# TensorE's order in the attention written out by hand up to block 12, and the residual's transposes three blocks late

## The chip, the cores and the metric

The kernel runs on one core of a Trainium2 chip. The metric is the device time of one execution in microseconds, as the median of several runs. A core has five engines, each with its own queue: TensorE (PE; its weight loads are shown apart as PEld), VectorE (DVE), ScalarE (ACT), GpSimd (POOL) and SyncE (SP), which issues nearly all DMAs. TensorE writes its results to PSUM[...]; VectorE and ScalarE read them from there.

## The reference

One transformer block on `x` of 2048 x 1024, in fp32, with one attention head of width 256 and a gated feed-forward part of width 2752:

```python
x = x + layernorm(attention(layernorm(x), Wqkv, bqkv, Wo, bo))
x = x + layernorm(ffn(layernorm(x), W_gate, W_up, W_down))

# attention
q, k, v = split(x @ Wqkv + bqkv)
out = softmax(q @ k.T / 16) @ v
return out @ Wo + bo
# ffn
return (silu(x @ W_gate.T) * (x @ W_up.T)) @ W_down.T
```

## The kernel before

Every fp32 operand of a matmul is held as a pair, a rounded high part and the low part that is left (`split`: a copy on ScalarE, line 109, and a subtraction on VectorE, line 110). A product of two such operands is three matmuls, hi·hi, hi·lo, lo·hi (`mm3`, lines 144 to 148). Where the output is narrow (256 columns, `attend`), hi·hi and hi·lo are one matmul of 512 columns (line 276) and lo·hi one of 256 (line 277).

The kernel has these stages. From 0 to about 155 us the rows of `x` are normalised, transposed, and multiplied to q, k and v; the last four `v_block`s come just after the first block's scores. Then the attention runs over 16 blocks of 128 query rows (the loop of line 899). After it comes the feed-forward part, all through line 605, in two halves of the rows, with Strassen-like sums of its operands; it fills the rest up to 1693 us.

In one pass of the loop, block `i` does this:

- `turn(i, j)`, j = 0 to 3: four transposes on TensorE (line 268) of the exponentials `p_s` into bank 4 or 7, then a `split` into `pT`.
- `scores(i + 1, j)`: six matmuls (lines 146 to 148) of the next block's query rows with 512 keys into bank j, and the row maximum on VectorE (line 251).
- `softmax(i + 1)`: small operations on VectorE, four exponentials on ScalarE (line 259) from banks 0 to 3 into `p_s`, the sum and its reciprocal (lines 260 and 261).
- `turn_o(i - 1)`: two transposes (line 285) of the block before's output into bank 5, and a `split` into `oTs`.
- `attend(i)`: 32 matmuls into bank 6; then ScalarE copies one half of the bank (line 279) and VectorE adds the other (line 280).
- `proj(i - 1)`: two halves of six matmuls each, the first into bank 5, the second into bank 7, each followed by an eviction on VectorE that scales and adds the bias (line 295).
- `xpose(i - 2)` for the first eight blocks (`EARLY`): eight transposes (line 347) of the finished rows into banks 6 and 5, a copy on ScalarE for each bank (line 349), and a store to `xT_d` (line 351).
- `residual(i - 1)` for the first eight blocks: bn_stats (line 116), aggregates (119, 120), a power on GpSimd (121), a normalisation on ScalarE (303), the addition of `x` (304), and the same once more for the second layernorm (308). The rows lie in three pairs of buffers (`pair`), used in turn.
- `first_sums` and `first_load` in later blocks load the transposed rows back (line 361) and form the feed-forward part's first operands (lines 384 and 407, 408).

The Python order of the calls isn't the order on the engines. A scheduler reorders all instructions by its own estimate of when each can run, under the data dependencies; only instructions marked with `tc.keep_in_program_order` keep their order among themselves on their engine. In the kernel before no attention matmul is marked, and the scheduler weaves pieces of `attend`, `scores`, `turn`, `proj` and `xpose` into each other. On each engine the woven order is then fixed; an instruction waits on semaphores of others. Buffers and banks are named by the kernel, so a bank that is written again waits for its last reader.

## Time and profile before

| | us |
|---|---|
| median of 3 runs (lowest to highest) | 1696.84 (1696.13 to 1699.03) |
| the profiled execution | 1695.4 |
| its span, first to last instruction | 1693.5 |
| mean granted TensorE clock | 0.996 |
| first transpose of `p_s` on TensorE | at 163.04 |
| last matmul of `attend(15)` begins | at 439.84 |
| last gap on TensorE between attention and feed-forward part ends | at 464.66 |

How to read its lines. On the page, busy time is given per engine with its share of the span and its count of instructions; the chain follows, from the last instruction backwards, what released each step. A line of the view by stretch has the stretch, its length, then for each engine the busy time and in brackets the instructions begun in it, then the granted clock, the share of the DMA engines and GB/s. A line of the waits has the waiting instruction, who released it, the sum of the idle time in us, how often, and the longest. A line of the timeline has start and duration in us, engine, source line, operation, output and input with shapes, count, and in brackets the idle time before it and who ended it. In all views a number of a line of the kernel (L276) is a number of the listing above; in the changed kernel the same lines stand eight or more further down.

### The profile page before, as it was taken

The numbers are of one execution on the slowest core, as the hardware profiler recorded it, in microseconds if no ns is written. First come the engines' busy times: TensorE is split into PE (matmuls) and PEld (weight loads), VectorE is DVE, ScalarE is ACT, GpSimd is POOL, SyncE is SP. The second block draws the span as 40 slices with busy tenths as digits, with TensorE's granted clock in tenths as the row PEclk, the third lists the DMA queues.
The fourth block names the chain that finished last, engine by engine and source line by source line (L and its number), as shares of the span: only waits on it lengthen the run. The fifth ranks groups of instructions, "written<-read, shape, count | busy, mean of one in ns | idle before, by whom it ended". The sixth has DMA issues, their size and how long they took to land.

```text
span 1693.5 us, 21093 instructions
## 1 busy us (share of the span) xinstructions
PE 1669.1 (99%) x7764; PEld 1385.6 (82%) x7764; DVE 1098.7 (65%) x1682; ACT 695.1 (41%) x1039; POOL 91.2 (5%) x118
## 2 busy tenths in 40 slices
PE   8999999999899999999999999999999999999997
PEld 6888887888688888888888888888888888888886
DVE  8643667667687777777578447966555665445458
ACT  3222445544544444444355444433333333344343
POOL 1000000000001111111000000100000000000001
PEclk9999999999999999999999999999999999999999
DMA  6221123335655666666567655633332223666654
GB/s 214 81 81 38 38 75 112 100 115 178 211 175 199 205 207 231 216 211 223 175 215 254 209 191 193 212 118 115 130 105 94 93 94 124 217 215 194 193 191 158
DMA packets 131014, 271.00 MB, mean 160 GB/s; under 512 B 13280, under 2 KB 29792, under 8 KB 130912
## 3 DMA queue, kind: packets, MB, share of 16 engines
q1 hardware_dynamic: 128176, 262.72, 46.5%
q10 hardware_dynamic: 2736, 6.95, 1.2%
q8 instruction: 60, 0.98, 0.2%
q14 instruction: 42, 0.34, 0.1%
HBM read 185.73 MB, written 83.89 MB: 159 GB/s over the span
## 4 chain that ended last, share of the span: by engine, by line
PE 94%; DVE 2%; issue 1%; DMA 1%; ACT 1%; POOL 0%; POOLq 0%; DVEq 0%; SPq 0%; ACTq 0%
PE bank L605 71%; PE bank L147 4%; PE bank L146 4%; PE bank L148 4%; PE bank L276 3%; PE bank L277 2%; PE bank L206 2%; PE bank L268 1%; PE bank L207 1%; PE bank L347 1%; PE bank L139 1%; DVE small L116 1%; PE bank L784 0%; PE bank L785 0%; DMA f<-x 0%
## 5 line engine op out<-in xcount | busy, mean ns | idle before, releaser
L605 PE MATMUL bank<-a 128*128 128x512 f32 x1164 | 274.2, 389 | 0.0
L605 PEld LDWEIGHTS bank<-a 128*128 128x128 f32 x1164 | 218.5, 188 | 45.4
L605 PE MATMUL bank<-xb,a 128*128 128x512 f32 x912 | 212.1, 389 | 0.0
L605 PEld LDWEIGHTS bank<-xb,a 128*128 128x128 f32 x912 | 171.1, 188 | 35.5
L110 DVE TENSOR_TENSOR a<-f2p,a 128x1024 fp32r<-128x1024 f32 (+2 forms) x133 | 134.6, 1012 | 57.7 <-ACT a L109 53.7
L109 ACT CAST a<-f2p 128x1024 fp32r<-128x1024 f32 (+2 forms) x133 | 117.5, 884 | 127.4 <-PE bank L605 103.9
L110 DVE TENSOR_TENSOR a<-f,a 128x1024 fp32r<-128x1024 f32 (+2 forms) x91 | 91.1, 1001 | 105.7 <-ACT a L109 103.7
L605 PE MATMUL bank<-wvo 128*128 128x512 f32 x612 | 149.6, 389 | 0.0
L605 PE MATMUL bank<-kx,a 128*128 128x512 f32 x612 | 146.3, 389 | 0.0
L605 PE MATMUL bank<-a,a 128*128 128x512 f32 x588 | 140.1, 390 | 0.9 <-ACT xi L661 0.9
L605 PEld LDWEIGHTS bank<-kx,a 128*128 128x128 f32 x612 | 114.8, 188 | 24.1 <-ACT a L109 0.3
L605 PEld LDWEIGHTS bank<-wvo 128*128 128x128 f32 x612 | 114.9, 188 | 23.9
L605 PEld LDWEIGHTS bank<-a,a 128*128 128x128 f32 x588 | 110.2, 188 | 24.6 <-ACT xi L661 1.4
L109 ACT CAST a<-f 128x1024 fp32r<-128x1024 f32 (+2 forms) x91 | 69.6, 764 | 139.3 <-PE bank L605 108.1
L618 DVE TENSOR_TENSOR p_s<-bank,p_s 128x512 f32<-128x512 f32 x96 | 65.1, 682 | 78.4 <-PE bank L605 43.2
L605 PE MATMUL bank<-a,wvo 128*128 128x512 f32 x444 | 106.2, 389 | 0.0
L605 PE MATMUL bank<-kx,wvo 128*128 128x512 f32 x420 | 100.1, 389 | 0.0
L276 PE MATMUL bank<-a,a 128*128 128x512 f32 x256 | 94.8, 403 | 4.2 <-ACT f L349 2.1
L110 DVE TENSOR_TENSOR wvo<-f,wvo 128x1024 fp32r<-128x1024 f32 (+1 forms) x52 | 60.7, 1168 | 56.8 <-ACT wvo L109 56.5
L605 PEld LDWEIGHTS bank<-a,wvo 128*128 128x128 f32 x444 | 83.3, 188 | 17.3
L605 PEld LDWEIGHTS bank<-kx,wvo 128*128 128x128 f32 x420 | 78.8, 188 | 16.4
L121 POOL TENSOR_TENSOR small<-small,mhalf 128x1 f32<-128x1 f32 x48 | 38.0, 792 | 702.6 <-DVE small L120 670.7
(245 smaller groups left out, 2772.5 us busy)
## 6 DMA issues: line engine op xcount, KB each, us to landing
f2p<-wgu SPq DMA_DIRECT2D x41, 512.0 KB, 5.3
f<-x SPq DMA_DIRECT2D x30, 512.0 KB, 3.9
hd_S<-p_s SPq DMA_DIRECT2D x60, 256.0 KB, 4.5
f<-wgu SPq DMA_DIRECT2D x22, 512.0 KB, 3.5
wr<-wgu SPq DMA_DIRECT2D x21, 512.0 KB, 5.7
f<-wd SPq DMA_DIRECT2D x20, 512.0 KB, 5.0
hd_A<-xi SPq DMA_DIRECT2D x40, 256.0 KB, 2.0
td_T<-f SPq DMA_DIRECT2D x40, 256.0 KB, 4.5
```

The source lines that it names most:

```text
L109: nc.scalar.copy(hi, src)
L110: (lo_engine or nc.vector).tensor_tensor(lo, src, f32(hi), ALU.subtract)
L116: b = nc.vector.bn_stats(s[:, 6 * i : 6 * i + 6], h)
L121: nc.gpsimd.tensor_tensor(s[:, 15:16], s[:, 14:15], mhalf, ALU.pow)
L146: nc.tensor.matmul(o, w[0], m[0], start=first, stop=False)
L147: nc.tensor.matmul(o, w[0], m[1], start=False, stop=False)
L148: nc.tensor.matmul(o, w[1], m[0], start=False, stop=last)
L206: nc.tensor.matmul(b, xg[:, c, 0, cols], wv_s[:, c, :, :].rearrange("p a f -> p (a f)"), start=(c == 0), stop=False)
L276: nc.tensor.matmul(b, p[:, k, 0, :], vt[:, k, :, :].rearrange("p h d -> p (h d)"), start=(k == 0), stop=False)
L277: nc.tensor.matmul(b[:, D:], p[:, k, 1, :], vt[:, k, 0, :], start=False, stop=(k == NKB - 1))
L605: one = nc.tensor.matmul(o, w[i], m[j], start=first and n == 0, stop=last and n == 2, skip_group_check=chained)
L618: nc.vector.tensor_tensor(o, a, b, op)
```

## The change

A marker `pin` is passed to the attention's matmuls and transposes. While `block[0]`, which the loop sets to `i`, is under 13, it marks them with `tc.keep_in_program_order`; in the last three passes it does nothing. (The scores of block 0 are never marked; those of block 13 are issued in pass 12 and are.) Three things move in the loop: `xpose` comes a block later and in front of `turn(i, 2)`, with its two banks exchanged; `turn_o` comes before the load of `x`; `q_load` moves from the start of the passes 4 and 8 to the middle of the passes 5 and 9. The second half of `proj` goes to bank 6 in place of bank 7. The name `pin` of the later code becomes `keep`. With this, TensorE's order in a block is: turns 0 and 1, the next scores 0 and 1, the transposes of `xpose(i - 3)`, turns 2 and 3, scores 2 and 3, `turn_o(i - 1)`, `attend(i)`, `proj(i - 1)`.

```diff
-    def mm3(o, w, m, first, last):
-
-        nc.tensor.matmul(o, w[0], m[0], start=first, stop=False)
-        nc.tensor.matmul(o, w[0], m[1], start=False, stop=False)
-        nc.tensor.matmul(o, w[1], m[0], start=False, stop=last)
+    def mm3(o, w, m, first, last, pin=lambda i: i):
+
+        pin(nc.tensor.matmul(o, w[0], m[0], start=first, stop=False))
+        pin(nc.tensor.matmul(o, w[0], m[1], start=False, stop=False))
+        pin(nc.tensor.matmul(o, w[1], m[0], start=False, stop=last))
...
+    ORDERED = NT - 3
+    block = [0]
+
+    def pin(i):
+        return tc.keep_in_program_order(i) if block[0] < ORDERED else i
+
+    free = lambda i: i
...
-            mm3(bank[j], (q[:, d, 0, cols], q[:, d, 1, cols]), (k[:, 0, :], k[:, 1, :]), d == 0, d == 1)
+            mm3(bank[j], (q[:, d, 0, cols], q[:, d, 1, cols]), (k[:, 0, :], k[:, 1, :]), d == 0, d == 1, pin if i else free)
...
-        for h, b in ((1, bank[5]), (0, bank[7])):
+        for h, b in ((1, bank[5]), (0, bank[6])):
             cols = slice(h * 512, h * 512 + 512)
             for d in range(2):
-                mm3(b, (oT[:, d, 0, :], oT[:, d, 1, :]), (wo_s[:, d, 0, cols], wo_s[:, d, 1, cols]), d == 0, d == 1)
+                mm3(b, (oT[:, d, 0, :], oT[:, d, 1, :]), (wo_s[:, d, 0, cols], wo_s[:, d, 1, cols]), d == 0, d == 1, pin)
...
     for i in range(NT):
         more = i + 1 < NT
-        if i % TB == 0 and TB <= i < NT - TB:
-            q_load(i // TB + 1)
+        block[0] = i
         turn(i, 0)
         turn(i, 1)
         if more:
             scores(i + 1, 0)
             scores(i + 1, 1)
+        if 3 <= i < EARLY + 3:
+            xpose(i - 3, *pair[(i - 3) % 3], (bank[5], bank[6]), pin)
         turn(i, 2)
         turn(i, 3)
         if more:
             scores(i + 1, 2)
             scores(i + 1, 3)
             softmax(i + 1)
+        if i > 0:
+            turn_o(i - 1)
+        if i % TB == 1 and TB < i < NT - TB:
+            q_load(i // TB + 1)
         if i < EARLY:
             nc.sync.dma_start(pair[i % 3][1], x[i * P : (i + 1) * P, :])
-        if i > 0:
-            turn_o(i - 1)
...
         attend(i)
         if i > 0:
             proj(i - 1)
-        if 2 <= i < EARLY + 2:
-            xpose(i - 2, *pair[(i - 2) % 3], (bank[6], bank[5]))
```

The transposes of `turn`, `turn_o` and `xpose` and the matmuls of `attend` get `pin(...)` around them in the same way.

More of the change, by code (lines that the diff above doesn't have):

```diff
@@ L267, in turn @@
             k = 4 * j + n
-            nc.tensor.transpose(b[:, n * P : (n + 1) * P], p_s[:, k * P : (k + 1) * P], ident)
+            pin(nc.tensor.transpose(b[:, n * P : (n + 1) * P], p_s[:, k * P : (k + 1) * P], ident))
         d = pT[i % 2][:, 4 * j : 4 * j + 4, :, :]
@@ L275, in attend @@
         for k in range(NKB):
-            nc.tensor.matmul(b, p[:, k, 0, :], vt[:, k, :, :].rearrange("p h d -> p (h d)"), start=(k == 0), stop=False)
-            nc.tensor.matmul(b[:, D:], p[:, k, 1, :], vt[:, k, 0, :], start=False, stop=(k == NKB - 1))
+            pin(nc.tensor.matmul(b, p[:, k, 0, :], vt[:, k, :, :].rearrange("p h d -> p (h d)"), start=(k == 0), stop=False))
+            pin(nc.tensor.matmul(b[:, D:], p[:, k, 1, :], vt[:, k, 0, :], start=False, stop=(k == NKB - 1)))
         o = o_s[i % 2]
@@ L284, in turn_o @@
         for d in range(2):
-            nc.tensor.transpose(b[:, d * P : (d + 1) * P], o_s[i % 2][:, d * P : (d + 1) * P], ident)
+            pin(nc.tensor.transpose(b[:, d * P : (d + 1) * P], o_s[i % 2][:, d * P : (d + 1) * P], ident))
         split(oTs[i % 2][:, :, 0, :], oTs[i % 2][:, :, 1, :], b.rearrange("p (d q) -> p d q", d=2))
@@ L339, in block_kernel, with xpose @@
         split(wo_s[:, d, 0, :], wo_s[:, d, 1, :], f4[d])
-    def xpose(t, a, b, banks):
+    def xpose(t, a, b, banks, pin=lambda i: i):
         for hf in range(2):
@@ L346, in xpose @@
                 cb = 4 * hf + j
-                nc.tensor.transpose(o[:, j * P : (j + 1) * P], a[:, cb * P : (cb + 1) * P], ident)
+                pin(nc.tensor.transpose(o[:, j * P : (j + 1) * P], a[:, cb * P : (cb + 1) * P], ident))
             s = b[:, hf * 512 : hf * 512 + 512]
@@ L399, in build_x @@
         split_x("T4", cb, r1[:, R])
-    pin = tc.keep_in_program_order
+    keep = tc.keep_in_program_order
     def split_later(dst, src):
-        pin(nc.scalar.copy(dst[:, :, 0, :], src))
-        pin(nc.vector.tensor_tensor(dst[:, :, 1, :], src, f32(dst[:, :, 0, :]), ALU.subtract))
+        keep(nc.scalar.copy(dst[:, :, 0, :], src))
+        keep(nc.vector.tensor_tensor(dst[:, :, 1, :], src, f32(dst[:, :, 0, :]), ALU.subtract))
     def first_load(cb, r1, r2):
@@ L743, in down_weights @@
         r1, r2 = f4[0:2]
-        pin(nc.vector.tensor_tensor(r2[:, R], r2[:, R], r1[:, R], ALU.subtract))
+        keep(nc.vector.tensor_tensor(r2[:, R], r2[:, R], r1[:, R], ALU.subtract))
         add(r1[:, R], r1[:, R], r1[:, L], ALU.subtract)
```

## The prediction

> **What bounds the kernel now.** I read four views in this order: the page's shares and its chain of waits, the busy time by stretch, TensorE's waits, and the timelines of TensorE, VectorE and ScalarE between 163 us (the first transpose of `p_s`) and 466 us (where the feed-forward part runs without gaps).

> ```profile
> PE 1669.1 (99%) x7764; PEld 1385.6 (82%) x7764; DVE 1098.7 (65%) x1682; ACT 695.1 (41%) x1039; POOL 91.2 (5%) x118
> ...
> PE 94%; DVE 2%; issue 1%; DMA 1%; ACT 1%; POOL 0%; POOLq 0%; DVEq 0%; SPq 0%; ACTq 0%
> ```

> TensorE sets the end. The number and size of its matmuls do not change, so the change can only add or remove gaps. The stretches show how little there is to win:

> ```profile
> 163.00:418.00 255.00, 250.97 (x1380) 211.41 (x1379) 169.75 (x342) 121.47 (x254) 12.99 (x32) 1.00 0.30 99
> 418.00:466.00 48.00, 43.37 (x198) 34.32 (x197) 35.12 (x47) 25.93 (x37) 0.00 (x0) 1.00 0.59 204
> ```

> The third column is TensorE: 4.0 us idle in the first stretch, 4.6 us in the second. Its waits there:

> ```profile
> PE bank L276 <- ACT f L349: 2.1, 3, 1.4
> PE bank L276 <- ACT a L109: 2.1, 2, 1.4
> ...
> PE bank L146 <- DVE oTs L110: 0.5, 1, 0.5
> ```

> A gap costs more than its idle time, because a matmul of 512 columns is drawn 0.39 us long but starts 0.2266 us after its predecessor (114.26 us for 504 in the chain). So I count start to start:

> ```profile
> 274.69 0.60 PE L347 MATMUL bank<-ident,f 128*128 128x128 f32 x4
> 275.12 0.60 PE L268 MATMUL bank<-ident,p_s 128*128 128x128 f32 x4
> 275.56 0.38 PE L285 MATMUL bank<-ident,f 128*128 128x128 f32 x2
> 277.37 0.50 PE L276 MATMUL bank<-a,a 128*128 128x512 f32 x1 [1.43 <-ACT f L349]
> ```

> Ten transposes at 0.11 us should take 1.1 us less the 0.08 us that the last of a group gives to the next matmul (202.25 to 202.60 for four, and 0.31 instead of 0.2266 for the matmul after); they took 2.68: 1.67 us lost. Summed this way, the gaps of at least 0.05 us before 412 us cost 6.0 us (at 176 to 179 us 1.34; 207 0.76; 222 0.26; 239 0.64; 259 to 261 0.89; 274 1.67; 293 to 296 0.47). From 436 to 466 us another 6.5 us are lost.

> [...] at 236.40 below, an addition stands behind an instruction that waited. [...] The change puts `proj`'s second half into the bank in which `attend` has just ended; that is my main term. [...]

> **The change part by part.** I compared the instruction orders of the two built programs; they carry no times.

> *Removed.* The order that the scheduler wove (`attend` cut into pieces, transposes between) goes up to block 12, and with it the places of the 6.0 us. In the fixed order the next softmax lies beside `attend` and `proj` (5.6 + 2.7 us), and `xpose`'s data are a block older. Gain 6.0 us; from 4 (some return elsewhere) to 8 (the small excess goes too: 784 matmuls at 0.0035 us is 2.8 us).

> *Fewer groups of transposes.* 81 groups become 49. Four transposes and the matmul after take 0.35 + 0.31 = 0.66 us, which is 4 x 0.109 + 0.2266; two take 0.13 + 0.32 = 0.45, which is 2 x 0.11 + 0.2266. So the price is per transpose, not per group: nothing.

> *Later loads.* `q_load` comes a block later and the load of `x` behind it on SP; both have some ten us before their reader in the next block (store 2.3 to 5.9 us and load 3.9 us, begun near 5 us of a block of 16.7 us). Nothing; up to 1 us.

> *The added wait: bank 6.* `attend(i)` ends in bank 6; `proj(i-1)` does half 1 in bank 5 (six matmuls, 1.36 us), then half 0 in bank 6. Its first matmul waits for the addition (line 280 before, 288 after), which follows ScalarE's copy (279, after 287). How fast it can be, from quiet engines:

> ```profile
> 390.48 0.28 PE L277 MATMUL bank<-a,a 128*128 128x256 f32 x1
> ...
> 390.79 0.37 ACT L279 COPY f<-bank 128x256 f32<-128x256 f32 x1 [4.07 <-PE bank L277]
> ...
> 391.20 0.42 DVE L280 TENSOR_TENSOR f<-bank,f 128x256 f32<-128x256 f32 x1 [0.50 <-ACT f L279]
> ...
> 391.75 0.39 PE L148 MATMUL bank<-wvo,oTs 128*128 128x512 f32 x1
> ...
> 392.18 0.75 DVE L295 SCALAR_TENSOR_TENSOR f<-bank,ys,bo_s 128x512 f32<-128x512 f32 x1 [0.56 <-PE bank L148]
> ```

> The bank is free at 391.62 + 0.06 and would be wanted at 391.98: 0.3 us of room. But in the changed program VectorE's queue has the eviction of half 1 (line 303, before 295) ahead of the addition in blocks 2, 4, 5, 6, 8 and 9, and in all but block 9 a bn_stats (116) between them as well. The eviction must wait for half 1's last matmul, so half 0 cannot start with it. The trace of before has one such case, and there nobody waited for the bank:

> ```profile
> 236.40 0.75 DVE L295 SCALAR_TENSOR_TENSOR f2p<-bank,ys,bo_s 128x512 f32<-128x512 f32 x1 [2.32 <-PE bank L148]
> 237.06 0.42 DVE L280 TENSOR_TENSOR f<-bank,f 128x256 f32<-128x256 f32 x1
> 237.39 0.69 DVE L116 BATCH_NORM_STATS2 small<-f2p 128x6 f32<-128x512 f32 x1
> 237.99 0.68 DVE L110 TENSOR_TENSOR a<-bank,a 128x512 fp32r<-128x512 f32 x1
> ```

> From the moment when half 0 wants to start: 0.20 until the eviction starts (391.98 to 392.18), 0.66 until the next may start (236.40 to 237.06), 0.60 for bn_stats (237.39 to 237.99), 0.42 for the addition, 0.06 to TensorE (207.89 to 207.95), and 0.1 for each small op of the softmax between. Block 2: 2.1; 4, 5, 6 and 8: 2.0 each; 9: 1.4. Sum 11.5 us, on the path because TensorE's next instruction is that matmul and the order is fixed. Bounds: 10 (no small ops) and 14 (ScalarE's copy late too: in blocks 4, 5 and 8 four exponentials and a 1.24 us activation stand ahead of it).

> *Block 10.* Four sums of `first_sums` (line 392) precede the addition on VectorE and wait for loads. Before, the first of them ran 8.34 us after `xpose`'s last copy (343.28 to 351.62). That copy ends about 5.3 us into the block, so the sums start near 13.6, take 4 x 0.6 and small ops, and the addition ends near 16.7 where 15.3 is wanted: 1.4 us (0 to 4).

> *Block 0.* `wo`'s two splits wait for the last `v_block` matmuls and stand on VectorE ahead of the evictions of the transposes; the fourth transpose group waits for bank 7, by the durations about 0.9 us (0 to 1). Blocks 3 and 7 have the addition first, after late exponentials: 0.1 each.

> *The tail.* Blocks 13 to 15 stay woven. By `attend(15)`'s end the new program has done 40 feed-forward matmuls and the old one 50; the other 10 (2.3 us) then cover waits of the 6.5 us. I take 2 us off (6.5 off to 2 on).

> Sum: 11.5 + 1.4 + 0.9 + 0.2 - 6.0 - 2.0 = +6.0 us. The profiled execution took 1695.4 us, 1.9 more than its span, so 1701.4; the median 1696.84 lies 1.4 above it, and with it the forecast is 1702.8.

> **The rivals.** (1) The tail absorbs the delay, so the time is not slower: the preparations between 436 and 466 us do not depend on TensorE's delay and all 6.5 us go. Then +1.5 us, 1698.3. For it: the chain there passes two DMA waits (5.20 and 4.52 us). Against: the buffers of those loads are freed by the same blocks. It decides from 4.6 us absorbed. (2) The fixed order wins: the lost 6.0, all of the tail's 6.5 and the 2.8 of small excess go, and the bank waits cost only their lower bound, 10: -4 to -5, 1692. Against: three bounds at once. (3) Late VectorE work pushes on: exponentials and loads in blocks 9 to 12 come late as well, 5 us more, 1708. For it: in a residual block VectorE has some 11 us of work in 16.7 us, and 1.24 us activations sit ahead of splits. (4) The order isn't kept as written: excluded, the built order shows it.

> **How the numbers follow.** Forecast 0.52, rival 1 0.23, rival 2 0.11, rival 3 0.14. 0.2% is 3.4 us, about what a measurement of this kernel can tell from no change. Slower takes rival 3 and nearly all of the forecast, 0.65; same takes rival 1 and the forecast's low edge, 0.23; faster 0.12. The range goes from 1695 (between rivals 1 and 2) to 1708 (rival 3); the forecast's own range is 1699 to 1706.

> **What would show it.** TensorE's waits: the proj matmul of line 146 released by VectorE's line 288, six times or more, near 2 us each, 9 us or more in all; the waits on line 357's copies (349 before) gone from the attention; VectorE idle before line 303 (a wait on line 148), with line 288 after it. I am wrong if line 288's waits sum to less than 4 us, or if the span between 418 and 466 us loses its gaps.

## The result, and the profile after

The changed kernel takes 1712.67 us (median of 5 runs, 1710.39 to 1715.57) against 1696.84 us of the kernel before (5 runs, 1695.99 to 1699.03). The ratio is 1.0091, with an interval of 1.0080 to 1.0102: slower by 15.8 us. The forecast was 1702.8 with a range of 1695 to 1708; the direction was right, the size lies outside the range. The profiled execution took 1710.6 us with a span of 1708.6 us, 15.1 more than before; the sums below are made against that. Only this run was profiled, and it is one of the two shortest. The granted clock listed for the five runs falls as they get longer, from 0.994 and 0.993 (1710.55 and 1710.39 us) to 0.990 (1715.57 us). A stretch of 3.41 us at half clock, of which more below, lowers that mean by 0.001 (3.41 / 2 in 1710 us), so the median run, at 0.991, probably holds more of them than the profiled one; that is an estimate.

The page and its chain say the same as before: the same 7764 matmuls, TensorE at the end, and a lower share of it.

```profile
PE 1673.3 (98%) x7764; PEld 1389.5 (81%) x7764; DVE 1097.9 (64%) x1682; ACT 693.5 (41%) x1039; POOL 91.2 (5%) x118
...
PE 94%; DVE 2%; DMA 2%; ACT 1%; issue 1%; POOL 0%; SPq 0%; POOLq 0%; DVEq 0%; ACTq 0%
```

The view by stretch shows where the time went:

```profile
163.00:418.00 255.00, 240.15 (x1296) 202.55 (x1295) 155.29 (x320) 113.08 (x238) 13.00 (x32) 0.98 0.28 90
418.00:466.00 48.00, 46.17 (x230) 37.70 (x230) 37.14 (x57) 24.40 (x41) 0.00 (x0) 1.00 0.54 187
```

In the attention's 255 us TensorE is now idle for 14.9 us where it was 4.0, begins 1296 matmuls and transposes where it began 1380, and its granted clock, 1.00 before, is 0.98. The second stretch is not comparable line by line, since the attention ends later in it. TensorE's waits name the causes:

```profile
PE bank L146 <- DVE f L288: 12.2, 7, 2.0
PE bank L276 <- DVE f L211: 2.7, 1, 2.7
```

The first is the wait for bank 6 (one of the kernel's eight tiles of 128 x 512 fp32 in PSUM, line 77) that the prediction was about: seven times, at 217, 253, 272, 293, 330, 350 and 368 us, which are blocks 2, 4, 5, 6, 8, 9 and 10. The waits on line 349's copies (357 now), 2.1 us before, are gone from the attention. Here is one of the seven, in block 5, from the timeline of PE, VectorE and ScalarE (lines left out where marked):

```profile
269.34 1.25 ACT L316 ACTIVATE f<-f,small 128x1024 f32<-128x1024 f32 x1
269.50 0.16 DVE L268 TENSOR_REDUCE ys<-ys 128x1 f32<-128x4 f32 x1 [2.85 <-ACT p_s L267]
...
269.73 0.39 PE L148 MATMUL bank<-wvo,oTs 128*128 128x512 f32 x1
270.16 0.75 DVE L303 SCALAR_TENSOR_TENSOR f<-bank,ys,bo_s 128x512 f32<-128x512 f32 x1 [0.50 <-PE bank L148]
270.47 0.38 ACT L287 COPY f<-bank 128x256 f32<-128x256 f32 x1
...
270.94 0.69 DVE L116 BATCH_NORM_STATS2 small<-f 128x6 f32<-128x512 f32 x1
271.55 0.41 DVE L288 TENSOR_TENSOR f<-bank,f 128x256 f32<-128x256 f32 x1
272.01 0.50 PE L146 MATMUL bank<-wvo,oTs 128*128 128x512 f32 x1 [1.90 <-DVE f L288]
...
273.28 0.60 PE L148 MATMUL bank<-wvo,oTs 128*128 128x512 f32 x1
273.68 1.91 PE L276 MATMUL bank<-ident,p_s 128*128 128x128 f32 x8
...
275.24 0.78 PE L146 MATMUL bank<-kx,qb 128*128 128x512 f32 x1
```

The reader sees the queue that the prediction described: the last matmul of proj's half 1 starts at 269.73, its eviction (L303) at 270.16, bn_stats (L116) at 270.94, and only then the addition that frees bank 6 (L288) at 271.55. Half 0 could have started at 269.96 (269.73 + 0.2266) and starts at 272.01. ScalarE's copy (L287) ended at 270.85 and was not the last.

The lower part shows something that the prediction did not have. From 273.30 to 276.71 us matmuls took twice as long: eight transposes take 1.56 us from start to start of what follows (273.68 to 275.24), where 8 x 0.109 less 0.08 gives 0.79. (The drawn durations end later than that; only starts are counted here.) The stretches that begin after the gaps of block 4 and of block 5 differ in one column, the granted clock:

```profile
252.90:256.20 3.30, 3.16 (x18) 2.68 (x19) 1.49 (x4) 1.00 (x2) 0.00 (x0) 1.00 0.00 0
273.40:276.80 3.40, 3.40 (x14) 2.91 (x13) 2.68 (x4) 1.17 (x2) 0.00 (x0) 0.51 0.03 5
```

After three of the seven gaps (blocks 5, 6 and 8) TensorE ran for 3.41 us at half clock, that is, at a granted clock of 0.50, from 273.30, 293.78 and 331.32 us. Counted from start to start, against 0.2266 us for a matmul of 512 columns and 0.109 for a transpose, that cost 1.6 us each time.

The second wait, in block 0, is larger than predicted. The transposes of `turn(0, 1)` go to bank 7, which holds the last `v_block`, and the addition that reads it out (L211) stands behind two splits on VectorE:

```profile
169.72 1.22 DVE L110 TENSOR_TENSOR wvo<-f,wvo 128x1024 fp32r<-128x1024 f32 x1
170.86 0.68 DVE L110 TENSOR_TENSOR a<-bank,a 128x512 fp32r<-128x512 f32 x1
171.46 0.41 DVE L211 TENSOR_TENSOR f<-bank,f 128x256 f32<-128x256 f32 x1
...
172.02 0.63 PE L276 MATMUL bank<-ident,p_s 128*128 128x128 f32 x4 [2.67 <-DVE f L211]
```

The balance of the two profiled executions, from start to start on TensorE:

| term | predicted, us | measured, us |
|---|---|---|
| gaps of the woven order, gone | -6.0 | -6.5 |
| bank 6 in blocks 2, 4, 5, 6, 8, 9 | 11.5 | 12.4 |
| bank 6 in block 10 | 1.4 | 1.6 |
| bank 6 in blocks 3 and 7 | 0.2 | 0.25 |
| block 0 | 0.9 | 2.9 |
| half clock after three gaps | none | 4.9 |
| tail (from 436 us) | -2.0 | -0.9 |
| after TensorE's last matmul | none | 0.4 |
| sum | +6.0 | +15.1 |

The last line but one is no wait of TensorE: the last matmul begins at 1683.66 us before and at 1698.35 after, 14.7 us later, and the span ends 15.1 later.

### The profile page after: what moved, and what is told of

Its sections match the earlier page's. It is cut to its first block, busy times and chain, and to the rows that moved or that the text cites. A ratio compares the mean times of both kernels' runs of the same rounds, so it can differ in the third digit from the quotient of the medians.

```text
span 1708.6 us, 21083 instructions
## 1 busy us (share of the span) xinstructions
PE 1673.3 (98%) x7764; PEld 1389.5 (81%) x7764; DVE 1097.9 (64%) x1682; ACT 693.5 (41%) x1039; POOL 91.2 (5%) x118
## 4 chain that ended last, share of the span: by engine, by line
PE 94%; DVE 2%; DMA 2%; ACT 1%; issue 1%; POOL 0%; SPq 0%; POOLq 0%; DVEq 0%; ACTq 0%
PE bank L613 70%; PE bank L146 4%; PE bank L148 4%; PE bank L147 4%; PE bank L284 3%; PE bank L276 2%; PE bank L285 2%; PE bank L206 1%; PE bank L355 1%; PE bank L207 1%; PE bank L139 1%; DVE small L116 1%; PE bank L792 0%; PE bank L793 0%; DMA f<-wgu 0%
## 5 line engine op out<-in xcount | busy, mean ns | idle before, releaser
L613 PE MATMUL bank<-a 128*128 128x512 f32 x1164 | 274.2, 389 | 0.0
L613 PEld LDWEIGHTS bank<-a 128*128 128x128 f32 x1164 | 218.5, 188 | 45.4
L613 PE MATMUL bank<-xb,a 128*128 128x512 f32 x912 | 212.5, 389 | 0.0
L613 PEld LDWEIGHTS bank<-xb,a 128*128 128x128 f32 x912 | 170.9, 188 | 35.4
L110 DVE TENSOR_TENSOR a<-f2p,a 128x1024 fp32r<-128x1024 f32 (+2 forms) x133 | 134.5, 1012 | 58.9 <-ACT a L109 55.0
L109 ACT CAST a<-f2p 128x1024 fp32r<-128x1024 f32 (+2 forms) x133 | 117.4, 884 | 130.7 <-PE bank L613 101.2
L110 DVE TENSOR_TENSOR a<-f,a 128x1024 fp32r<-128x1024 f32 (+2 forms) x91 | 91.5, 1005 | 105.9 <-ACT a L109 103.7
L613 PE MATMUL bank<-wvo 128*128 128x512 f32 x612 | 149.6, 389 | 0.0
L613 PE MATMUL bank<-kx,a 128*128 128x512 f32 x612 | 146.9, 390 | 1.6 <-ACT kx L415 1.1
L613 PE MATMUL bank<-a,a 128*128 128x512 f32 x588 | 140.0, 389 | 0.9 <-ACT xi L669 0.9
L613 PEld LDWEIGHTS bank<-kx,a 128*128 128x128 f32 x612 | 114.6, 188 | 26.2 <-ACT kx L415 1.5
L613 PEld LDWEIGHTS bank<-wvo 128*128 128x128 f32 x612 | 114.9, 188 | 23.9
L613 PEld LDWEIGHTS bank<-a,a 128*128 128x128 f32 x588 | 110.2, 188 | 24.6 <-ACT xi L669 1.3
L109 ACT CAST a<-f 128x1024 fp32r<-128x1024 f32 (+2 forms) x91 | 69.6, 765 | 141.9 <-PE bank L613 106.9
L613 PE MATMUL bank<-a,wvo 128*128 128x512 f32 x444 | 106.2, 389 | 0.0
L613 PE MATMUL bank<-kx,wvo 128*128 128x512 f32 x420 | 100.1, 389 | 0.0
L613 PEld LDWEIGHTS bank<-a,wvo 128*128 128x128 f32 x444 | 83.3, 188 | 17.3
L110 DVE TENSOR_TENSOR wvo<-f,wvo 128x1024 fp32r<-128x1024 f32 (+1 forms) x52 | 60.8, 1169 | 56.0 <-ACT wvo L109 55.4
L613 PEld LDWEIGHTS bank<-kx,wvo 128*128 128x128 f32 x420 | 78.8, 188 | 16.4
```

The source lines that it names most:

```text
L109: nc.scalar.copy(hi, src)
L110: (lo_engine or nc.vector).tensor_tensor(lo, src, f32(hi), ALU.subtract)
L613: one = nc.tensor.matmul(o, w[i], m[j], start=first and n == 0, stop=last and n == 2, skip_group_check=chained)
```

## The experiments

Theory A was that the waits for bank 6 and for block 0's bank, and the half clock that came after three of the five longer ones (1.90 to 1.96 us), are the whole loss, and that the fixed order is a gain once the banks are free. Its rivals: the order itself costs time; bank 6 alone costs it; the half clock has nothing to do with the gaps. Line numbers are those of the changed kernel. Each kernel was compared with runs of the kernel before on the same chip (1696.8 to 1697.2 us).

**Another bank for proj's second half (bank 1).** Bank 1 holds a quarter of the next block's scores, which the second of the four exponentials reads while `attend` runs.

```diff
-        for h, b in ((1, bank[5]), (0, bank[6])):
+        for h, b in ((1, bank[5]), (0, bank[1] if block[0] < ORDERED else bank[6])):
```

> proj's second half goes to bank 1 in the marked passes; all else as in the changed kernel. Theory A (the loss is the wait for bank 6, and the slow clock follows from its gaps): the waits of line 146 on line 288 go (14.3 us counted start to start), no stretch of half clock is left in the attention (4.9 us), and bank 1 is free in time because its exponentials end before the first half of proj does. 1712.7 - 19.2 = 1693.5, with 1692 to 1697 allowed for the tail. Theory B (the fixed order and the late transposes cost by themselves): 1703 or more, the gaps return at other places.

Measured: 1692.66 us (1690.14 to 1695.94), ratio 0.9975 (0.9968 to 0.9981), span 1689.7. No wait on line 288 is left:

```profile
163.00:418.00 255.00, 252.33 (x1392) 215.76 (x1391) 169.91 (x346) 121.62 (x256) 13.08 (x32) 0.99 0.31 101
171.28:174.69 3.41, 2.89 (x9) 2.54 (x10) 1.49 (x4) 0.99 (x2) 0.00 (x0) 0.50 0.49 154
```

The 2.7 us of idle time in the first stretch are block 0's wait. One point of the expectation failed: a stretch of half clock is left, the second line, right after that wait. (In the changed kernel the same wait brought none; the last section says why. It brought one in the two kernels with bank 7 and with the addition first, too, from 172.6 and 172.9 us.) One bank, with the rest of the change kept, takes 20 us off and makes the kernel faster than before. So most of the loss is in the bank, and with this bank the order is a gain. Bank 1 in the woven order was not tried.

**The bank of before (bank 7) in the fixed order.**

```diff
-        for h, b in ((1, bank[5]), (0, bank[6])):
+        for h, b in ((1, bank[5]), (0, bank[7])):
```

> proj's second half goes to bank 7, as before the change; the order stays marked. Theory A: no waits on line 288, but the next block's second group of transposes (bank 7, 0.4 us after proj's end) now waits for the eviction of that half: 0.2 + 0.75 + 0.06 - 0.44 = 0.6 us in each of 12 blocks, 7 us in all, too short for the clock to drop. 1700, 1697 to 1704. Theory B: as in the changed kernel or slower, 1710 or more.

Measured: 1704.87 us, ratio 1.0052 (1.0037 to 1.0067). TensorE's waits:

```profile
PE bank L276 <- DVE f L303: 5.2, 7, 1.4
PE bank L276 <- DVE f L211: 2.7, 1, 2.7
PE bank L276 <- ACT a L109: 2.1, 3, 0.7
```

With the old bank the wait moves to the next block: its transposes into bank 7 (L276) come right after proj and wait for the eviction (L303). Eleven such places lose about 10 us from start to start, over the 7 expected, and the time lies just above the expected range. None of these waits (1.4 us at most) was followed by half clock. So in a fixed order without free room bank 7 is no way out either: with the bank of before, the fixed order and the moves make the kernel 8.0 us slower.

**No block marked.** All other parts of the change are kept, and the scheduler weaves as before.

```diff
-    ORDERED = NT - 3
+    ORDERED = 0
```

> Nothing is marked (the scheduler orders all blocks), but the moved calls and bank 6 stay. Theory A: the scheduler weaves other matmuls between the end of attend and the second half of proj, so bank 6 costs little: 1694 to 1700, as before the change. Theory B: the moved calls and the bank carry part of the loss without any marking: 1703 to 1712.

Measured: 1697.36 us, ratio 1.0007 (0.9998 to 1.0015). The moved `xpose`, `turn_o` and `q_load`, and bank 6, cost nothing that could be measured when TensorE's order isn't fixed. The trace has one stretch of half clock, and it follows two shorter gaps (1.01 and 0.53 us, waits on the feed-forward part's splits), not one long one:

```profile
442.40:445.80 3.40, 1.86 (x7) 0.97 (x6) 2.88 (x5) 3.17 (x4) 0.00 (x0) 1.00 0.87 231
445.80:449.20 3.40, 3.40 (x9) 2.56 (x8) 3.09 (x5) 1.92 (x4) 0.00 (x0) 0.50 1.02 392
```

**Bank 6 alone in the kernel before.**

```diff
-        for h, b in ((1, bank[5]), (0, bank[7])):
+        for h, b in ((1, bank[5]), (0, bank[6])):
```

> The kernel before with proj's second half in bank 6 in place of 7 and nothing else of the change. Theory A (the wait comes from the bank together with the fixed order: a scheduler that knows of the bank puts other work between attend and the second half): the same as before within 2 us, 1697 (1695.5 to 1699), waits on line 280 under 3 us in all. Rival B (the bank alone makes the wait): six or more waits of 1 us or more on line 280 and 1704 or more.

Measured: 1697.88 us, ratio 1.001 (1.0001 to 1.0018). There is no wait on line 280 (288 in the changed kernel) among TensorE's; the first ones in the attention are those of the woven order:

```profile
PE bank L276 <- ACT f L349: 2.1, 5, 0.7
...
PE bank L276 <- DVE f L295: 0.9, 1, 0.9
PE bank L276 <- ACT a L109: 0.7, 1, 0.7
```

So bank 6 and the moves cost next to nothing without the fixed order (about 1 us at most in the medians), while the fixed order costs 15.8 us with bank 6, 8.0 with bank 7 and nothing with bank 1. What costs is the wait for a bank in an order that can't go round it.

**The addition ahead of the eviction on VectorE.** The two operations are marked too, so that they keep the program's order.

```diff
-        nc.vector.tensor_tensor(o, b[:, D:], o, ALU.add)
+        pin(nc.vector.tensor_tensor(o, b[:, D:], o, ALU.add))
...
-            nc.vector.scalar_tensor_tensor(a[:, cols], b, ys[i % 4][:, 13:14], bo_s[:, cols], ALU.mult, ALU.add)
+            pin(nc.vector.scalar_tensor_tensor(a[:, cols], b, ys[i % 4][:, 13:14], bo_s[:, cols], ALU.mult, ALU.add))
```

> Bank 6 stays; VectorE's addition after attend and proj's evictions are marked too, so that the addition stands ahead of the first half's eviction. Theory A, with VectorE's queue as the cause: the waits on line 288 shrink to what ScalarE's copy leaves (it ends late behind exponentials and a 1.25 us activation): about 1.4 us in blocks 4, 5, 8 and 9, 1.2 in block 2, 1.3 in block 10, little elsewhere, 8.5 us instead of 14.3; with gaps of 1.4 us the clock does not drop (4.9 us more). 1702, 1699 to 1706. If the clock drops all the same: 1707. If the queue's order does not matter: 1712.

Measured: 1705.57 us, ratio 1.0057 (1.0042 to 1.0072), at the upper end of what was expected. The waits on line 288 are still seven but shorter, and the timeline of block 5 says why they do not go:

```profile
270.99 1.25 ACT L316 ACTIVATE f<-f,small 128x1024 f32<-128x1024 f32 x1
...
272.12 0.38 ACT L287 COPY f<-bank 128x256 f32<-128x256 f32 x1
272.53 0.42 DVE L288 TENSOR_TENSOR f<-bank,f 128x256 f32<-128x256 f32 x1 [1.03 <-ACT f L287]
...
273.01 0.50 PE L146 MATMUL bank<-wvo,oTs 128*128 128x512 f32 x1 [1.21 <-DVE f L288]
```

With VectorE's queue out of the way, the same bank waits for ScalarE's: its copy (L287) stands behind the exponentials and a normalisation of 1.25 us (L316). It is so in the other blocks too: VectorE waited for line 287 before line 288 eight times, 9.2 us in all. Two queues held the bank, and the prediction's upper bound for the term (ScalarE's copy late too) was the second. After these shorter gaps (1.21 to 1.68 us) there is no half clock. The one after block 0's wait, about 1.6 us, was not in the expectation and is part of why the time came out at its upper end.

**Block 0's bank.** The last four `v_block`s go to banks 5 and 6.

```diff
-        v_block(NG - 1, tb, bank[6 + tb % 2])
+        v_block(NG - 1, tb, bank[5 + tb % 2])
```

> The last four v_blocks go to banks 5 and 6 in place of 6 and 7, so that the second group of transposes of block 0 (bank 7) has no eviction to wait for. Theory A (the 2.7 us wait of line 276 on line 211 stands on TensorE's path, the rest of the changed kernel is as it is): that wait is gone, the bank-6 waits on line 288 stay at about 12 us in seven places, time 1712.7 - 2.9 = 1709.8 (1708 to 1711.5, by how many clock drops fall after the gaps). Rival B (another wait on VectorE's late splits of block 0 takes its place): a new wait of 1.5 us or more before 180 us, 1711.5 to 1713.

Measured: 1710.34 us (1708.79 to 1711.66), ratio 1.008 (1.0066 to 1.0094). The wait on line 211 is gone. The profiled execution is no shorter than the changed kernel's (span 1708.8), because four gaps instead of three were followed by half clock in it, and block 7 has a bank-6 wait while block 6's is shorter (12.8 us in eight places); the median is 2.3 us below the changed kernel's, where 2.9 were expected, but the two intervals overlap, so the gain in time isn't settled by this run alone.

**Both banks moved.** Both one-line edits (banks 1, and 5 and 6).

> The last four v_blocks in banks 5 and 6, and proj's second half in bank 1 while the order is marked. Theory A (the two banks' waits are separate and both on the path, and the clock drop near 172 us came from the block-0 gap): the sum of both edits, 1692.7 - 2.9 - 1.3 = 1688.5 (1687 to 1690.5); no wait on line 288 or 211 over 0.3 us, no half-clock stretch between 163 and 418 us. Rival B (the wait in block 0 returns elsewhere): 1691 to 1693.

Measured: 1689.42 us (1687.49 to 1690.24), ratio 0.9957 (0.9944 to 0.9971), span 1685.4, 8.1 below the kernel before. By stretch:

```profile
163.00:418.00 255.00, 255.00 (x1415) 218.24 (x1415) 170.21 (x348) 121.67 (x257) 13.00 (x32) 1.00 0.31 101
418.00:466.00 48.00, 43.89 (x198) 34.80 (x197) 39.90 (x54) 27.59 (x39) 0.00 (x0) 1.00 0.64 219
```

TensorE is busy in all of the 255 us, at full clock. No half clock is left there, as expected. This is what the fixed order is worth with these banks: the attention's loss of 6.5 us in the woven order (gaps of at least 0.05 us) goes to nothing. About 1 us more comes from shorter gaps in the tail; the small excess hardly moves (4.0 and 3.8 us between 163 and 436 us). How much of this the new banks would have gained in the woven order was not tried.

**All 16 blocks marked,** on top of both banks.

```diff
-    ORDERED = NT - 3
+    ORDERED = NT
```

> As the version with both banks moved, but all 16 blocks marked. Theory A (leaving the last three blocks to the scheduler lets feed-forward matmuls fill waits of the tail): slower than that version by 1 to 5 us, with longer waits between 418 and 466 us. Rival B (the tail waits on the feed-forward part's preparations, whichever order its last attention blocks have): within 1 us of it.

Measured: 1686.19 us (1685.92 to 1688.07), ratio 0.994 (0.9927 to 0.9954), span 1684.1. Theory A of this run has fallen: the last three blocks are not better off with the scheduler. From 425 to 478 us the gaps sum to 4.2 us, and to 5.5 with 13 blocks marked. The three waits of 1.5 (L613 on L416), 1.0 (L613 on L415) and 0.5 us (again on L416) have gone, and these stand there:

```profile
PE bank L146 <- DVE oTs L110: 1.2, 1, 1.2
PE bank L613 <- ACT p_s L647: 1.0, 1, 1.0
```

Rival B (within 1 us) isn't shown either, since the medians lie 3.2 us apart. Whether it is faster than the version with 13 blocks is not settled, since the two intervals overlap at their ends; both are faster than the kernel before.

**A longer gap.** One more bn_stats of 0.6 us on VectorE after proj's first half, with its result unused, in the changed kernel.

```diff
+            if h and i < EARLY:
+                nc.vector.bn_stats(ys[i % 4][:, 14:20], a[:, cols])
```

> The changed kernel with one more bn_stats of 0.6 us on VectorE after the first half of proj, its result not used. It lengthens the bank-6 gap to about 2.6 us in blocks 2, 5, 6 and 8 and leaves about 1.3 us in blocks 4, 7 and 9. Theory A (TensorE's clock halves for 3.41 us when about 2 us or more of idle time fall into one stretch of a fixed 3.41 us grid): a half-clock stretch follows each of the four long gaps that has over 1.95 us in one stretch of the grid (2 to 4 of them), and none of the short ones; waits on line 288 sum to 15 us; time 1715.5 (1712 to 1719). Rival B (the half clock has another cause, such as load, and met the gaps by chance): half-clock stretches also without a gap of 2 us ahead, or none after most of the long gaps.

Measured: 1713.85 us (1711.52 to 1716.48), ratio 1.0101 (1.0088 to 1.0115), waits on line 288 of 15.0 us in eight places. The long gaps before 217.55, 273.71, 293.27 and 332.56 lasted 2.56, 2.49, 2.55 and 2.49 us. The clock after each, or at its second part, by stretch:

```profile
218.50:221.90 3.40, 3.40 (x14) 2.90 (x13) 2.12 (x4) 1.03 (x2) 0.00 (x0) 0.50 0.00 0
273.10:276.40 3.30, 2.69 (x16) 2.35 (x17) 1.51 (x4) 0.56 (x2) 0.00 (x0) 1.00 0.00 0
293.60:297.00 3.40, 3.40 (x12) 2.79 (x11) 0.97 (x2) 0.15 (x1) 0.00 (x0) 0.50 0.00 0
331.10:334.40 3.30, 1.84 (x10) 1.53 (x11) 1.55 (x4) 0.00 (x0) 0.00 (x0) 1.00 0.02 5
```

Two of the four were followed by half clock, and it is those that theory A names. The granted clock falls at 218.48 and at 293.58, 75.1 us apart, 22 times 3.413, so a grid can be laid through them. The idle time of the gap before 217.55 has 2.48 us in one stretch of the grid, that before 293.27 has 2.55; the grid cuts the gap before 273.71 into 1.88 and 0.61, and that before 332.56 into 1.05 and 1.44. Block 0's gap of 2.67 us is cut into 1.44 and 1.23, and no half clock follows it. None of the short gaps (1.18 to 1.40 us) was followed by half clock. The time came out 1.7 us below the expected value, which had counted on three such stretches; in the profiled execution there were two.

**The transposes two blocks late,** with both banks moved.

```diff
-        if 3 <= i < EARLY + 3:
-            xpose(i - 3, *pair[(i - 3) % 3], (bank[5], bank[6]), pin)
+        if 2 <= i < EARLY + 2:
+            xpose(i - 2, *pair[(i - 2) % 3], (bank[5], bank[6]), pin)
```

> The version with both banks moved, its transposes of the residual two blocks late instead of three, at the same place of the fixed order. In the trace of before the second layernorm of a block ended 13.0 and 15.6 us after its last proj eviction began; the transposes would stand 3.6 us after the end of proj. Theory A (the third block of delay is what the fixed order needs): TensorE waits 4 to 10 us for line 316 in eight blocks, 1745 (1725 to 1770). Rival B (the delay is not needed, the layernorm chain is quicker when nothing else is in its way): waits under 1 us each, 1689 to 1697.

Measured: 1773.88 us, ratio 1.0457 (1.0436 to 1.0478), span 1773.1. The third block of delay is needed: TensorE waits for the second layernorm in all eight blocks,

```profile
PE bank L355 <- ACT f L316: 45.3, 6, 7.6
PE bank L355 <- ACT f2p L316: 15.0, 2, 7.6
```

7.5 us each. These 60.3 us were in the range expected; the total was not. The span is 87.7 us above that with three blocks' delay, and the granted clock from 163 to 418 us is 0.85 in place of 1.00. This expectation left the half clock out just as the prediction had. Counted from start to start, matmuls at half clock account for about 21 of the other 27 us up to 436 us. The tail loses about 9 us more, with a wait of 4.3 us on line 415 that is followed by half clock once more; the rest are small differences the other way.

## Why the prediction was wrong, point by point

*What bounds the kernel.* Right: TensorE sets the end. The counting from start to start holds, and the balance above closes to within 0.1 us with it. But the statement that the change can only add or remove gaps was the first error: after three of the gaps the matmuls ran slower too, with 0.42 to 0.43 us from one start to the next for 512 columns in place of 0.2266.

*Removed gaps.* Right: -6.0 predicted, -6.5 measured, and with the banks moved nothing returns.

*Groups of transposes and later loads at nothing.* Right for the sum. That the moves cost nothing was shown where TensorE's order isn't fixed (ratio 1.0007), and in the fixed order with both banks moved, where TensorE never waits from 163 to 418 us.

*The wait for bank 6.* Right in mechanism, place and nearly in size. In block 5 the eviction started 0.20 us after half 0 could have started, a small operation of the softmax 0.66 later, bn_stats 0.12 after that, and it took 0.61 to the addition. The matmul that restarts starts its successor 0.34 us later in place of 0.2266; this 0.11 us was missing in each of them, and is most of the 0.9 us by which six blocks exceeded the 11.5. Block 9 had no bn_stats and lost 1.5, as said (1.4).

*Block 10.* 1.6 against 1.4 us, as said.

*Block 0.* The step that put "about 0.9 us" on the fourth transpose group failed. The second group uses the same bank 7, comes earlier, and waits for the last `v_block`'s addition; VectorE does a split of 1.22 and one of 0.68 before it. It cost 2.9 us. The order of VectorE was known; what failed was the choice of the writer: the prediction asked about a later writer of the bank in the fixed order, not about the first.

*The tail.* The step that gave 2 us failed in size: 0.9 us came. Ten more feed-forward matmuls were indeed left to cover, but the waits of 1.1, 0.5 and 1.5 us on the feed-forward part's splits, 0.2 on one of the attention's and 0.9 us on line 669 stay. Whether their inputs came late because the attention did was not tried.

*The half clock.* The sum had no such term. In the changed kernel the granted clock was 0.50 for 3.41 us from 273.30, 293.78 and 331.32 us; these are 20.48 and 37.55 us apart, 6 and 11 times 3.413. In the 3.41 us before each of the three TensorE had 1.90, 1.96 and 1.90 us of idle time. This is the step whose failure cost most: the prediction priced a gap by its length and put what follows it at nothing. This term is 4.9 of the 9.1 us that the sum was short; block 0 is 2.0, the tail 1.1, bank 6 1.2 (0.9, block 10's 0.2 and block 3's 0.05), the end after the last matmul 0.4, and the removed gaps 0.5 the other way.

*The rivals.* The first (the tail absorbs) and the second (the order wins) did not happen in the changed kernel; of the second, the lost 6.0 us do go once the two banks are free, but not all of the tail's. The third (late VectorE work pushes on, 1708) had the nearest number but not the cause: in blocks 9 to 12 TensorE waits only in blocks 9 and 10, for bank 6, and the sum had both.

*The range.* Its upper end came from the price of late work in four blocks. It left no room for a loss that comes after a gap (1.6 us after each of three). This missing term and three mis-sized ones of the same sign (block 0, bank 6, the tail) went past it together.

## What to carry to other kernels

Writing an engine's order out by hand takes away the scheduler's way round a bank that is not free yet. So before fixing the order, follow for every bank who reads it last and what stands ahead of that reader on its queue, from the first block on; here two one-line changes of bank turned a loss of 15.8 us into a gain of 7.7 (1697.15 to 1689.42). And price a gap on TensorE not only at its length: look at the granted clock after it (here three of five gaps of 1.90 to 1.96 us cost 1.6 us each on top, the other two nothing).
